# Query and output projections of a two-layer transformer on one core: eleven unit passes computed as seven half products of 128 columns, with the weights' sums kept in DRAM and loaded per visit

## The chip, the cores and the metric

The kernel runs on one core of a Trainium2 chip. The metric is the device time of one execution in microseconds (us). Five engines work side by side, each on its own list of instructions in program order: TensorE (PE, with its weight loads listed apart as PEld), VectorE (DVE), ScalarE (ACT), GpSimd (POOL) and SyncE (SP), which here only issues DMAs. They wait for one another through semaphores.

## The reference

2048 tokens (32 sequences of 64) with 512 features go through two conditioned layers, all in float32. Cut to what matters here:

```python
# layer 0
h = ada_rms(x, cond, ln1_w, ln1_tw)
q = (h @ Wq.T)  ; k = h @ Wk.T ; v = h @ Wv.T        # 8 query heads of 64, one key/value head
ctx = softmax(rope(q) @ rope(k).T / 8) @ v            # within each sequence of 64
x = x + ctx @ Wo.T                                    # Wq, Wo: 512 x 512
h = ada_rms(x, cond, ln2_w, ln2_tw)
x = x + (silu(h @ Wg.T) * (h @ Wu.T)) @ Wd.T          # 512 -> 2048 -> 512
# layer 1
h = layernorm(x) * (1 + scale(cond)) + shift(cond)
q = h @ Wq.T ; c = h @ Wkd.T ; k = c @ Wku.T ; v = c @ Wvu.T   # 16 heads of 32, 4 key/value heads
x = x + softmax(rope(q) @ rope(k).T / sqrt(32)) @ v @ Wo.T     # Wq, Wo: 512 x 512
```

Four projections are square: q and o of both layers. They are what the change touches.

## The kernel before

**Units and blocks.** The tokens are cut into NU = 8 units of UT = 256. Activations are kept with the features on the partitions: x of a unit is a tile [128, 4, 256], four chunks of 128 features. The MLP runs over five blocks of units, BLOCKS = ((0), (1, 2), (3, 4), (5, 6), (7)). While the MLP of one block runs, layer 0's attention of the next block's units and layer 1's attention of finished units run beside it.

**The square projections before.** `project` (L626) computes 128 output features of one unit: four matmuls, one for each chunk of the contraction, each with weights [128, 128] and 256 moving columns, summed in PSUM. A whole square projection takes 16 of them. Each float32 matmul leaves two records in the trace, so 32 records. The weights (`wqkv`, `wo0`, `wq1`, `wo1`) are loaded once and stay in SBUF. `query(i)` in `attention0` and in `attention1` projects half of the queries into one PSUM bank, and `rotate` (L634 to L637) makes the rotary embedding from that bank: v (L634) and u (L635) on DVE, a shuffle of v (L636) on DVE, and their sum qT (L637) on POOL. `output` projects the context cT, and adds each half to x on DVE (L682; for the last two units of layer 1, whose order is written by hand, chunk by chunk in L676).

**The MLP's half products.** The MLP's three matrices are already multiplied with seven half products in place of eight (Strassen's scheme in Winograd's form): the weights of a slice are cut into quarters, the moving tile into two halves of tokens by two halves of features, and seven products of sums of quarters replace the eight products of quarters. `multiply` (L1048) issues the four EARLIER products P1, P6, P5, P7 and later the three LATER ones, P2, P3, P4. The PSUM regions of the early products are read between the two, in `partial`: ACT copies one (e, L1063), DVE makes u (L1064) and w (L1065); the later products are then added onto what stays in the banks. For one unit the moving width is 128 columns, for a pair of units 256. The sums of the weights' quarters are made once, in block 0, on DVE (L331 to L333) and POOL (L334), stored to DRAM (`sums`) and loaded again in all later blocks, four slices ahead of use, all on SP's queue. L331 to L334 wait for the raw weights' loads ("stays<-in_wmlp").

**What sets the order.** At the start and at the end the order of PE's work is written by hand (the strings FIRST and LAST). In between, pieces of the jobs (an MLP block, layer 0's attention of the next units, the chain of layer 1's attentions of units 0 to 5, called `behind`) are interleaved by a planner: each piece yields a cost and a latency, and the planner takes the job that is the least advanced. The program order on every engine is fixed when the kernel is built. In this middle part attention has two PSUM banks ("at"), the MLP six ("gu"). The layer-1 attention of unit 6 starts in the last block, and it ends together with unit 7's in the hand-written end.

**Norms.** The root and its reciprocal (L567 on ACT, L568 on DVE), h from x (L609, L613 on POOL, L622 on DVE), and hc, the sums of h's quarters that the MLP's moving side needs (L850 to L853 on DVE), stand between a unit's output projection and its MLP.

Of the kernel before, what the change touches and what calls it, by code (L numbers as in the profile page):

```python
# [10 lines left out]
F32 = mybir.dt.float32  # L11
I32 = mybir.dt.int32
AF = mybir.ActivationFunctionType
ALU = mybir.AluOpType
# [32 lines left out]
WARM = 11  # L47
STAY = 13854 - 4 * 128 + 4 * 128 + 4 * 256 + 128 + 4 * 7 * 256 + 4 * 7 * 256
FIRST = "aaaaaaa bb a mm aa bb a bbb aa b mm a bb r aa a m b a bi m b i a | b".replace(" ", "")
# [4 lines left out]
H2 = 4  # L54
MODS = 4

LAST = "aa b aa b iii b aa ii b bb bbb aaaa a b a b aaaa bbbb bb bbbb".replace(" ", "")
# [74 lines left out]
def two_blocks(ctx: ExitStack, tc: tile.TileContext, a: dict, out: bass.AP):  # L132
# [9 lines left out]
    def bank(tag, name):  # L142
        return psum.tile([P, 512], F32, tag=tag, name=name, bufs=BANKS[tag])
# [3 lines left out]
    class Regions:  # L147


        def __init__(self, name, n, ht):  # L150
            self.n, self.ht, self.per = n, ht, 512 // (n * ht)
            self.banks = [
                bank("gu", f"{name}_{i}").rearrange("p (r c t) -> p r c t", c=n, t=ht) for i in range(4 // self.per)
            ]

# [13 lines left out]
    def abank(name):  # L169
        tags = homes["now"]  # L170
        homes["n"] += 1
        return bank(tags[homes["n"] % len(tags)], name)
# [4 lines left out]
    def fixed(shape):  # L177
        n, i = int(np.prod(shape[1:])), stays["at"]
        stays["at"] += n
        assert stays["at"] <= STAY  # L180
        t = stays["all"][:, i : i + n]
        if len(shape) == 2:
            return t
        names = "abc"[: len(shape) - 1]
        return t.rearrange(f"p ({' '.join(names)}) -> p {' '.join(names)}", **dict(zip(names, shape[1:])))
# [69 lines left out]

    wqkv = [fixed([P, KC, 384]), fixed([P, KC, 256])]
    wo0 = fixed([P, KC, D])
    wq1 = fixed([P, KC, D])
    wkd = fixed([P, KC, LAT])
    wkv1 = fixed([P, 2, P])  # L260
    wo1 = fixed([P, KC, D])

# [73 lines left out]
    def done_with(kind, what):  # L336
# [11 lines left out]
        else:  # L348
            load_part(kind, n + MW)

    mods = []

# [13 lines left out]
    load_x(0)  # L366
    for i, w in enumerate(wqkv):
        nc.sync.dma_start(w, a[f"wqkv{i}"])
    load_x(1)
    load_mod(1)  # L370
    nc.sync.dma_start(wo0, a["wo0"])
    first_loads.close()
# [251 lines left out]
    def project(ps, w, cols, h):  # L624
        for k in range(KC):
            nc.tensor.matmul(ps, w[:, k, cols], h[:, k, :], start=(k == 0), stop=(k == KC - 1))  # L626

    def rotate(dst, src, cos, sin, shape, name):

        u, v = (  # L630
            work(tag, [P, 512], f"{tag}_{name}")[:, : shape[1] * shape[2]].rearrange("p (c t) -> p c t", t=shape[2])
            for tag in "uv"
        )
        nc.vector.tensor_tensor(v, src, sin, ALU.mult)  # L634
        nc.vector.tensor_tensor(u, src, cos, ALU.mult)  # L635
        nc.vector.stream_shuffle(v, v, OTHER)  # L636
        nc.gpsimd.tensor_tensor(dst, u, v, ALU.add)  # L637
# [26 lines left out]

    def output(u, cT, w, name, last=False, fine=False):

        x = x_units[u]
        for h in range(2):
            po = abank(f"po_{name}_{h}").rearrange("p (c t) -> p c t", c=2)
            for c in range(2):  # L670
                o = 2 * h + c
                if fine and c:
                    po = abank(f"po_{name}_{h}_{c}").rearrange("p (c t) -> p c t", c=2)
                project(po[:, c], w, slice(o * P, (o + 1) * P), cT)
                if fine:
                    nc.vector.tensor_tensor(x[:, o], x[:, o], po[:, c], ALU.add)  # L676
                    nc.sync.dma_start(out[u][:, o], x[:, o])
                    yield 1.7, 0.0
            if fine:
                continue  # L680
            part = slice(2 * h, 2 * h + 2)
            nc.vector.tensor_tensor(x[:, part], x[:, part], po, ALU.add)  # L682
            yield 3.4, 2.0 * h
            if last:
                nc.sync.dma_start(out[u][:, part], x[:, part])
# [3 lines left out]
    def attention0(u, room):  # L689
# [4 lines left out]
        def query(i):  # L694

            q = abank(f"q0_{u}_{i}").rearrange("p (c t) -> p c t", c=2)
            for c in range(2):
                project(q[:, c], wqkv[i], slice(c * P, (c + 1) * P), h)
            two = [P, 2, UT]

            def turn(cos, sin):
                cos, sin = (t.unsqueeze(1).to_broadcast(two) for t in (cos, sin))
                rotate(qT[:, 2 * i : 2 * i + 2], q, cos, sin, two, f"q0_{u}_{i}")

            return turn

        def keys_values():
            kv = abank(f"kv0_{u}")
            project(kv[:, :UT], wqkv[0], slice(2 * P, 3 * P), h)
            return kv  # L710

        norm = rms(u, s0a, h, room, f"a{u}")
        yield next(norm)
# [20 lines left out]
        qT = tile4(room, "qT", f"qT0_{u}")  # L734
        turn = turn or query(0)
        turn(cos, sin)
        yield 0.0 if lean else 3.4, 0.0

# [20 lines left out]

        query(1)(cos, sin)  # L760
        yield 3.4, 0.0

# [61 lines left out]
        if not lean:  # L824
            contexts([0, 1])
            yield 1.1, 2.5
        yield from output(u, cT, wo0, f"0_{u}")

# [29 lines left out]
    def attention1(u, room):  # L858
# [34 lines left out]
        yield 0.43, 5.5 if slim else 9.0  # L893

        lat = abank(f"lat_{u}")
        project(lat[:, :UT], wkd, slice(0, LAT), h)
# [6 lines left out]

        def query(i):
            q = abank(f"q1_{u}_{i}")
            for c in range(2):
                project(q[:, c * UT : (c + 1) * UT], wq1, slice((2 * i + c) * P, (2 * i + c + 1) * P), h)
                if lean and c == 0:
                    yield 1.7, 0.0
            many = [P, 2 * US, S]  # L910
            rotate(
                qT[:, 2 * i : 2 * i + 2].rearrange("p c (b s) -> p (c b) s", s=S),
                q.rearrange("p (c s) -> p c s", s=S),
                cos.unsqueeze(1).to_broadcast(many),
                sin.unsqueeze(1).to_broadcast(many),
                many,
                f"q1_{u}_{i}",
            )

        def keys_values():  # L920
# [28 lines left out]

        queries = [query(i) for i in range(2)]  # L950
        if early:
# [82 lines left out]
        else:  # L1034
            contexts([0, 1], pTs)
            yield 1.7, 2.0
        yield from output(u, cT, wo1, f"1_{u}", True, lean)

# [198 lines left out]
    rest = [ahead, Job(turning(), 1.0)]  # L1237
    for w, key in ((wq1, "wq1"), (wkd, "wkd"), (wkv1, "wkv1"), (wo1, "wo1")):
        nc.sync.dma_start(w, a[key])
# [86 lines left out]
def _lay(w):  # L1326

    return np.ascontiguousarray(w.T.reshape(-1, P, w.shape[0]).transpose(1, 0, 2))


def _quarters(w, down):


    if down:
        q = w.reshape(2, 2 * P, 2, NP, P).transpose(3, 4, 0, 2, 1)
    else:
        q = w.reshape(2, NP, P, 2, 2, P).transpose(1, 5, 0, 3, 4, 2)
    return q.reshape(NP, P, 4, 2 * P)[:, :, [0, 1, 3, 2]]

# [64 lines left out]
```

## Time and profile before

| | us |
|---|---|
| median of 3 runs (lowest, highest) | 1000.67 (998.11, 1001.54) |
| the profiled execution | 1000.52 |
| its span in the trace | 998.7 |
| TensorE busy | 975.1 |
| VectorE busy | 530.1 |
| GpSimd busy | 428.2 |
| ScalarE busy | 302.0 |

DMA queues moved 132.23 MB in the span, and 16 DMA engines were busy for 39.5% of it. The granted clock of TensorE was 0.997 of full speed.

How to read what follows. A row of groups has line, engine, operation, tiles and shapes, the number of records, then busy us and mean ns of one, then the idle time of the engine just before them and what ended most of it. Matmuls overlap their neighbours, so a mean per record is longer than the distance from one to the next (the pitch); the pitch is read from unbroken runs in the chain of work that ended last, whose pieces have start, length and what ran. A window's row gives the busy time of PE, PEld, DVE, ACT and POOL in a stretch, the clock, the DMA engines' busy share and GB/s. "stays" is the name of the tiles that are kept for the whole kernel, weights above all; "po", "q", "kv", "lat", "gu" and "down" are PSUM banks.

Holes of TensorE before 240 us are ended by several things; the largest of the waits of PE by its releaser are 5.2 us for "issue" and 2.8 us for DVE's "stays" of L332, both ahead of MLP products.

### The profile page before, as it was taken

The numbers are of one execution on the slowest core, as the hardware profiler recorded it, in microseconds if no ns is written. First come the engines' busy times: TensorE is split into PE (matmuls) and PEld (weight loads), VectorE is DVE, ScalarE is ACT, GpSimd is POOL, SyncE is SP. The second block draws the span as 40 slices with busy tenths as digits, with TensorE's granted clock in tenths as the row PEclk, the third lists the DMA queues.
The fourth block names the chain that finished last, engine by engine and source line by source line (L and its number), as shares of the span: only waits on it lengthen the run. The fifth ranks groups of instructions, "written<-read, shape, count | busy, mean of one in ns | idle before, by whom it ended". The sixth has DMA issues, their size and how long they took to land.

```text
span 998.7 us, 17463 instructions
## 1 busy us (share of the span) xinstructions
PE 975.1 (98%) x6710; PEld 852.4 (85%) x6710; DVE 530.1 (53%) x1119; ACT 302.0 (30%) x560; POOL 428.2 (43%) x439
## 2 busy tenths in 40 slices
PE   8899988999999999999999999999999999999998
PEld 7788988888888888887888888888788889999986
DVE  5658787654373442655246372455334643654274
ACT  4453233223214210225214251222313330423132
POOL 3336257335433334435343352454325343844252
PEclk9999999999999999999999999999999999999999
DMA  7837376624222445223232234333323335745401
GB/s 269 310 117 239 130 248 196 208 92 134 69 69 80 137 139 173 90 80 110 78 108 88 73 132 138 115 106 106 96 86 105 132 109 168 246 149 190 138 1 43
DMA packets 82642, 132.23 MB, mean 132 GB/s; under 512 B 8832, under 2 KB 48512, under 8 KB 82176
## 3 DMA queue, kind: packets, MB, share of 16 engines
q1 hardware_dynamic: 82560, 131.12, 39.5%
q8 instruction: 53, 0.87, 0.4%
q14 instruction: 29, 0.24, 0.1%
HBM read 114.31 MB, written 16.78 MB: 131 GB/s over the span
## 4 chain that ended last, share of the span: by engine, by line
PE 87%; DMA 4%; DVE 3%; ACT 1%; POOL 1%; issue 1%; SPq 1%; POOLq 0%; DVEq 0%; ACTq 0%
PE gu L1048 38%; PE down L1048 17%; PE po L626 11%; PE q L626 10%; DMA stays<-in_wmlp 2%; PE pp L661 2%; PE sc L974 2%; PE lat L626 1%; PE kv L626 1%; ACT cT L815 1%; PE cx L805 1%; PE cx L1005 1%; PE sc L784 1%; DMA mod<-in_mod 1%; PE tab L494 1%
## 5 line engine op out<-in xcount | busy, mean ns | idle before, releaser
L1048 PE MATMUL gu<-h,stays 128*128 128x256 f32 (+1 forms) x1280 | 258.5, 340 | 5.9 <-issue 5.2
L1048 PEld LDWEIGHTS gu<-h,stays 128*128 128x128 f32 x1280 | 208.0, 191 | 30.4 <-issue 7.4
L1048 PE MATMUL down<-stays 128*128 128x256 f32 (+1 forms) x1120 | 208.4, 339 | 0.3 <-DVE stays L332 0.3
L1048 PE MATMUL gu<-hc,stays 128*128 128x256 f32 (+1 forms) x960 | 195.4, 338 | 2.8 <-DVE stays L332 2.8
L1048 PEld LDWEIGHTS down<-stays 128*128 128x128 f32 x1120 | 177.2, 190 | 22.4 <-issue 3.6
L1048 PEld LDWEIGHTS gu<-hc,stays 128*128 128x128 f32 x960 | 157.4, 191 | 18.4 <-DVE stays L332 3.0
L626 PE MATMUL q<-h,stays 128*128 128x256 f32 x480 | 110.7, 384 | 0.0
L626 PE MATMUL po<-cT,stays 128*128 128x256 f32 x480 | 107.9, 380 | 1.0 <-ACT cT L815 0.8
L1104 POOL TENSOR_TENSOR stays<-gate,stays 128x768 f32<-128x768 f32 (+1 forms) x40 | 53.8, 1346 | 114.7 <-DVE stays L1093 103.2
L626 PEld LDWEIGHTS po<-cT,stays 128*128 128x128 f32 x480 | 90.3, 190 | 14.4 <-ACT cT L815 2.4
L626 PEld LDWEIGHTS q<-h,stays 128*128 128x128 f32 x480 | 91.4, 192 | 12.6
L1063 ACT COPY e<-gu 128x256 f32<-128x256 f32 (+1 forms) x80 | 26.2, 328 | 172.5 <-PE gu L1048 169.7
L637 POOL TENSOR_TENSOR qT<-u_q,v_q 128x512 f32<-128x512 f32 x30 | 38.2, 1275 | 86.1 <-DVE v_q L636 82.9
L656 POOL TENSOR_TENSOR p<-p,sm 128x512 f32<-128x512 f32 x40 | 41.5, 1057 | 72.3 <-DVE sm L655 66.0
L682 DVE TENSOR_TENSOR x<-x,po 128x512 f32<-128x512 f32 x28 | 19.2, 686 | 90.7 <-PE po L626 90.7
L1064 DVE TENSOR_TENSOR u<-e,gu 128x256 f32<-128x256 f32 (+1 forms) x80 | 28.6, 358 | 53.2 <-ACT e L1063 53.0
L613 POOL TENSOR_TENSOR h<-x,stays 128x1024 f32<-128x1024 f32 x12 | 23.1, 1929 | 68.4 <-DVE x L682 38.4
L1105 POOL TENSOR_TENSOR stays<-stays 128x512 f32<-128x512 f32 (+1 forms) x40 | 45.0, 1126 | 2.9
L568 DVE RECIPROCAL stays<-stays 128x256 f32<-128x256 f32 (+1 forms) x23 | 35.4, 1540 | 19.7 <-ACT stays L567 19.5
L1065 DVE TENSOR_TENSOR w<-u,gu 128x256 f32<-128x256 f32 (+1 forms) x80 | 29.1, 364 | 30.8 <-PE gu L1048 29.6
L1151 POOL TENSOR_TENSOR x<-x,c 128x256 f32<-128x256 f32 x16 | 12.1, 758 | 74.3 <-DVE c L1138 74.3
L1093 DVE TENSOR_TENSOR gate<-gu,u 128x512 f32<-128x512 f32 (+1 forms) x40 | 23.3, 582 | 32.8 <-PE gu L1048 32.5
(230 smaller groups left out, 1266.2 us busy)
## 6 DMA issues: line engine op xcount, KB each, us to landing
stays<-sums SPq DMA_DIRECT2D x96, 384.0 KB, 3.0
stays<-in_wmlp SPq DMA_DIRECT2D x120, 256.0 KB, 2.9
stays<-in_wmlp SPq DMA_DIRECT2D x120, 128.0 KB, 2.5
stays<-sums SPq DMA_DIRECT2D x96, 128.0 KB, 2.3
sums<-stays SPq DMA_DIRECT2D x24, 384.0 KB, 3.8
mod<-in_mod SPq DMA_DIRECT2D x8, 512.0 KB, 6.3
x<-in_x SPq DMA_DIRECT2D x8, 512.0 KB, 6.2
a<-in_wmlp SPq DMA_DIRECT2D x24, 128.0 KB, 3.8
```

What stands on the lines that cost most here:

```text
L568: nc.vector.reciprocal(r, r)
L613: nc.gpsimd.tensor_tensor(by_seq(h), by_seq(x), per_seq(s, u), ALU.mult)
L626: nc.tensor.matmul(ps, w[:, k, cols], h[:, k, :], start=(k == 0), stop=(k == KC - 1))
L637: nc.gpsimd.tensor_tensor(dst, u, v, ALU.add)
L656: nc.gpsimd.tensor_tensor(p8, p8, sm.unsqueeze(2).to_broadcast(wide), ALU.mult)
L1048: nc.tensor.matmul(ps[REGION[p]][:, c], w[:, slot, cols], moving, start=opening and ps.opens(p, c, k), stop=p in LATER, skip_group_check=True,
L1063: nc.scalar.copy(e, ps[0])
L1064: nc.vector.tensor_tensor(u2, e, ps[1], ALU.add)
L1065: nc.vector.tensor_tensor(w2, u2, ps[2], ALU.add)
L1093: nc.vector.tensor_tensor(c12_21, ps.late_pair()[:, :, 0], u2.to_broadcast([P, 2, ht]), ALU.add)
L1104: e.tensor_tensor(act[:, 2:5], gate[:, 1:4], act[:, 2:5], ALU.mult)
L1105: e.tensor_tensor(act[:, 0:4:2], act[:, 2:4], act[:, 1:3], ALU.subtract)
```

## The change

The queries' and the output's projections of layer 0 for units 3 to 7, and of layer 1 for units 0 to 5, are computed as seven half products of 128 moving columns: five and six unit passes with two projections each, 22 projections. The rest keep the 256-column form. A halved projection is two output halves with 7 products of 2 matmuls each, 28 matmuls of 128 columns in place of 16 of 256.

- `halves_of` makes four half sums of the moving tile, three on DVE and one on POOL.
- `halved_products` issues the early products of both output halves, one "at" bank each, with `partial` after each, yields, and then issues the late products. `halved_queries` puts the four quarters into qT (one on DVE from w and P7, one by an ACT copy, a pair on DVE), and `rotate` then reads qT in place of the PSUM bank. `halved_output` adds the quarters onto x, partly on DVE and partly on POOL.
- The four matrices no longer stay in SBUF. Two rings of two tiles [128, 7, 256] hold seven quarters and sums of one matrix each. A *visit* is a stretch of units that use a matrix in a ring: ring 0 has q0 for units 0 to 3, po0 for unit 3, and then q0 and po0 of units 4 to 7 in turn; ring 1 has po0 for units 0 to 2, then q1 and po1 of units 0 to 5 in turn; at the end po1 of units 6 and 7 goes to ring 0 and their q1 to ring 1.
- At a matrix's first halved use, `square_sums` makes its sums: three additions on DVE and one on POOL for each of two halves. When that visit is done, `square_done` stores them to DRAM (896 KB for each half), and each later visit loads 896 KB for each half, issued on SP right after the last late product of the ring's previous visit. Raw loads, of 512 KB, are for first visits and unhalved uses.
- The keys' and values' weights of layer 0 are a tile of their own, `wkv0`.

In DMAs: 36 loads of 896 KB and 8 stores of 896 KB are added; 1024 KB and wqkv loads of the four matrices go, and raw loads of 512 KB come in their place.

The core of the diff:

```diff
+HALVED = (3, 6)
...
-    wqkv = [fixed([P, KC, 384]), fixed([P, KC, 256])]
-    wo0 = fixed([P, KC, D])
-    wq1 = fixed([P, KC, D])
+    wkv0 = fixed([P, KC, P])
...
-    wo1 = fixed([P, KC, D])
+    square = {ring: [fixed([P, 7, 2 * P]) for i in range(2)] for ring in "01"}
...
+    ORDER = ("q0", "po0", "q1", "po1")
+    visits = {"0": [("q0", (0, 1, 2, 3)), ("po0", (3,))], "1": [("po0", (0, 1, 2)), ("q1", (0,)), ("po1", (0,))]}
+    for u in range(4, NU):
+        visits["0"] += [("q0", (u,)), ("po0", (u,))]
+    for u in range(1, HALVED[1]):
+        visits["1"] += [("q1", (u,)), ("po1", (u,))]
+    visits["0"].append(("po1", (6, 7)))
+    visits["1"].append(("q1", (6, 7)))
...
+    def halved(what, u):
+        return u >= HALVED[0] if what[-1] == "0" else u < HALVED[1]
+
+    def load_square(ring, n, i):
+        if n >= len(visits[ring]):
+            return
+        what, units = visits[ring][n]
+        t = square[ring][i]
+        if what in summed_yet and halved(what, units[-1]):
+            nc.sync.dma_start(t, summed[what][:, i])
+        else:
+            nc.sync.dma_start(t[:, 3:7], a["square"][ORDER.index(what), i])
...
+    def square_done(what, u, i):
+        ring, n = visit_of[what, u]
+        if u == visits[ring][n][1][-1]:
+            if halved(what, u) and (what, i) not in summed_yet:
+                summed_yet.add((what, i))
+                nc.sync.dma_start(summed[what][:, i], square[ring][i])
+                if i:
+                    summed_yet.add(what)
+            load_square(ring, n + 1, i)
+
+    def square_sums(what, u):
+
+        if what not in summed_yet:
+            for i in range(2):
+                t = square_of(what, u, i)
+                nc.vector.tensor_tensor(t[:, 0], t[:, 6], t[:, 5], ALU.add)
+                nc.vector.tensor_tensor(t[:, 1], t[:, 0], t[:, 3], ALU.subtract)
+                nc.vector.tensor_tensor(t[:, 2], t[:, 3], t[:, 6], ALU.subtract)
+                nc.gpsimd.tensor_tensor(t[:, 6], t[:, 4], t[:, 1], ALU.subtract)
...
+    def halves_of(h, name):
+
+        b11, b12, b21, b22 = (h[:, r, t] for r in (slice(0, 2), slice(2, 4)) for t in (slice(0, HT), slice(HT, UT)))
+        ts = work("half", [P, 4, 2, HT], f"half_{name}", 2)
+        t1_, t2_, t3_, t4_ = (ts[:, k] for k in range(4))
+        nc.vector.tensor_tensor(t1_, b12, b11, ALU.subtract)
+        nc.gpsimd.tensor_tensor(t3_, b22, b12, ALU.subtract)
+        nc.vector.tensor_tensor(t2_, b22, t1_, ALU.subtract)
+        nc.vector.tensor_tensor(t4_, b21, t2_, ALU.subtract)
...
+    def halved_products(what, u, of, early, late):
+
+        pieces = [(0, CHUNKS[k], k) for k in range(2)]
+        some = []
+        for i in range(2):
+            ps = Regions(f"{what}_{u}_{i}", 1, HT, abank)
+            multiply(ps, EARLIER, True, square_of(what, u, i)[:, 0:4], of, pieces)
+            u2, w2 = partial(ps, ("pe", "pu", "pw"), f"{what}_{u}_{i}", 1, HT)
+            early(i, w2[:, 0], ps[3][:, 0])
+            some.append((ps, u2))
+        yield 3.6, 2.0
+        for i, (ps, u2) in enumerate(some):
+            multiply(ps, LATER, False, square_of(what, u, i)[:, 4:7], of, pieces)
+            square_done(what, u, i)
+            late(i, ps[0][:, 0], ps.late_pair()[:, :, 0], u2.to_broadcast([P, 2, HT]))
+        yield 2.7, 0.0
+
+    def halved_queries(what, u, h, qT, turn):
+
+        quarters = [qT[:, 2 * i : 2 * i + 2].rearrange("p c (h t) -> p (c h) t", t=HT) for i in range(2)]
+
+        def early(i, w2, p7):
+            nc.vector.tensor_tensor(quarters[i][:, 3], w2, p7, ALU.add)
+
+        def late(i, c11, pair, u2):
+            nc.scalar.copy(quarters[i][:, 0], c11)
+            nc.vector.tensor_tensor(quarters[i][:, 1:3], pair, u2, ALU.add)
+            turn(i)
+
+        yield from halved_products(what, u, halves_of(h, f"{what}_{u}"), early, late)
+
+    def halved_output(what, u, cT):
...
+        def early(i, w2, p7):
+            c22 = work("pc", [P, HT], f"pc_{what}_{u}_{i}")
+            nc.vector.tensor_tensor(c22, w2, p7, ALU.add)
+            nc.gpsimd.tensor_tensor(quarters[i][:, 3], quarters[i][:, 3], c22, ALU.add)
+
+        def late(i, c11, pair, u2):
+            to = quarters[i]
+            nc.vector.tensor_tensor(to[:, 1:3], to[:, 1:3], pair, ALU.add)
+            nc.vector.tensor_tensor(to[:, 0], to[:, 0], c11, ALU.add)
+            nc.gpsimd.tensor_tensor(to[:, 1:3], to[:, 1:3], u2, ALU.add)
+
+        of = halves_of(cT, f"{what}_{u}")
+        yield 0.0, 2.0
+        yield from halved_products(what, u, of, early, late)
+        yield 0.0, 2.5
```

## The prediction

> **What bounds the kernel now.** I read the busy times first, then the shares of the chain that ended last, then the pieces of that chain in order of time, the time by stretches, and what TensorE waited for. From the page, the span, the busy times, the chain's shares and the two groups that the change replaces:
>
> ```profile
> span 998.7 us, 17463 instructions
> ...
> PE 975.1 (98%) x6710; PEld 852.4 (85%) x6710; DVE 530.1 (53%) x1119; ACT 302.0 (30%) x560; POOL 428.2 (43%) x439
> ...
> PE 87%; DMA 4%; DVE 3%; ACT 1%; POOL 1%; issue 1%; SPq 1%; POOLq 0%; DVEq 0%; ACTq 0%
> ...
> L626 PE MATMUL q<-h,stays 128*128 128x256 f32 x480 | 110.7, 384 | 0.0
> L626 PE MATMUL po<-cT,stays 128*128 128x256 f32 x480 | 107.9, 380 | 1.0 <-ACT cT L815 0.8
> ```
>
> TensorE (PE) is idle for 998.7 − 975.1 = 23.6 us only. Less PE work is therefore less time, unless new waits take its place. A mean per record (384 ns) overlaps its neighbours, so it is no price; the pitch is. That is read from unbroken pieces of the chain (start, us, what):
>
> ```profile
> 47.77 7.19 PE po L626 x32
> ...
> 79.30 10.73 PE gu L1048 x96
> ...
> 142.43 6.91 PE po L626 x32
> ```
>
> A projection of 256 moving columns is 16 matmuls, two records each: 32 records in 6.91 us, 0.216 us each. The MLP's half products of one unit have 128 columns: 96 records in 10.73 us, 0.1118 us each. Half of 0.216 would be 0.108, so a short record pays 4 ns more than its share.
>
> Where are the 23.6 us? The windows give, for a stretch, its length, then busy us of PE, PEld, DVE, ACT and POOL, the clock, the DMA share and GB/s:
>
> ```profile
> 150.00:165.00 15.00, 11.87 (x98) 11.49 (x97) 9.55 (x26) 6.57 (x11) 13.77 (x16) 0.96 0.52 169
> 165.00:180.00 15.00, 14.72 (x105) 13.94 (x104) 14.93 (x22) 3.05 (x6) 5.86 (x8) 0.92 0.84 259
> 160.00:240.00 80.00, 77.08 (x476) 68.87 (x476) 50.39 (x97) 23.33 (x37) 34.52 (x35) 0.98 0.51 164
> 320.00:400.00 80.00, 80.00 (x399) 69.61 (x398) 31.00 (x56) 13.65 (x24) 32.06 (x30) 1.00 0.44 142
> 880.00:940.00 60.00, 60.00 (x549) 57.22 (x548) 26.09 (x73) 16.04 (x39) 22.23 (x29) 1.00 0.56 185
> ```
>
> From 240 to 940 us PE has no hole worth naming, with DVE busy for 39% (31.00 of 80) to 43% (26.09 of 60). The holes lie ahead of 240 us, and the worst at the border of block 0 and block 1, where DVE is full (14.93 of 15).
>
> **The change part by part.**
>
> 1. *PE work.* A halved projection has 28 matmuls, 56 records: 56 × 0.1118 = 6.26 us instead of 32 × 0.216 = 6.91, a gain of 0.645 us. Queries and outputs are halved in 5 units of layer 0 and 6 of layer 1: 22 projections, **−14.2 us**. If a short record cost only half (0.108), it would be 0.86 each, −19 us; that end I hold unlikely, as no MLP row shows it. The other end is a pitch of 0.1235 (6.91/56), where nothing is left; no unbroken row of 128 columns is near it.
>
> The row above is the answer to a rule that speaks against the change: the Trainium skill (TensorE: Matmul & The Clock Gate, section "LDWEIGHTS (loading the stationary operand)") prices a weight load by its columns alone, about 107 ns for 128, however few columns move. By it the 24 loads (in records) that each projection gains would cost 24 × 107 = 2.6 us if they showed; the 96 records in 10.73 us say that they lie beside the matmuls but for the 4 ns.
>
> 2. *DVE.* Prices by shape: an addition of 128 columns from PSUM 0.28 us (L1064, L1065), of 256 columns 0.42, of 256 columns with both inputs in SBUF 0.43 (L850) to 0.63 (L333). Halved queries add three half sums (1.3 us) and, for each of two column halves, u, w, c22 and the pair (0.28 × 3 + 0.42 = 1.26): 3.8 us. Outputs add 1.3 + 2 × (1.26 + 0.28) = 4.4 and lose two x+=po (L682) of 0.686: 3.0. Eleven of each is 75 us, and 24 weights' sums at 0.57 (L331 to L333) are 14: DVE goes from 530 to about 620 us, 63% of the span. POOL gains some 11 × (0.8 + 3.4) + 8 × 0.81 = 53 us (L1106, L334, L1155), ACT 66 copies × 0.264 = 17 us. In the middle of the run this is hidden by PE; by itself 0. Three places are not:
>
> 3. *The border of blocks 0 and 1.* The six q1 sums (6 × 0.57 = 3.4 us) and unit 3's three half sums (1.3) come before the reciprocal, h and hc of block 1 in DVE's program; L331 to L333 of the next MLP weights are behind them too. The raw q1 halves (2 × 512 KB) and stores of 896 KB go to SP ahead of the MLP's loads, whose "stays" already end waits here (159.71, 3.40 us). DVE has 5.4 us free at 150 to 165 and none at 165 to 180. Bounds: 0 (all fits into the free part) and 4.7 + 6.2 (a 512 KB load in line, by x's row) = 11. I take **+3**, the 4.7 less a part that fits. The six q0 sums (3.4 us) sit after the first angles at 14 us; PE's clock and POOL's L613 set that stretch, bounds 0 and 3.4, I take **+0.5**.
>
> 4. *From early to late products.* Both banks of the attention wait while ACT copies, DVE makes u and w, and other pieces run on PE. In program order the least that stands between is 1.8 us, usually 2.2 to 5; the need is 0.26 + 3 × 0.28 = 1.1 us. It fits, unless a reciprocal (L568, 1749 ns) or a softmax's 0.68 us row is ahead on DVE. An output's P6 also waits for two half sums (0.86 us) after cT; P1 and the piece put between cover that, except in units 3 and 7. Bounds 0 and 22 × 0.65 (all of the gain); I take **+2.5**, a tenth of a us each.
>
> 5. *Loads.* 36 sums of 896 KB and 8 stores are 40 MB on 132, so 51% of the DMA engines' time instead of 39.5%. A ring is loaded again while PE works 30 us and more on other things; only between po0(3) and q0(4) (about 10 us) and po1(5) and q1 of the last pair (about 8.5) is it tight. The nearest rows are 8.6 us (1024 KB wo) and 6.2 (512 KB): bounds 0 and about 3 us for each; I take **+1** in all. SP waits in line for the last late product; the MLP's loads behind it are four slices ahead, which hides some us. If that cover is gone each visit pays what a late load pays (2.8 to 4.6 us on the chain); I take 0.
>
> 6. *Order.* The planner's order shifts by pieces' costs (3.6 + 2.7 against 6.8), which may open or close holes: ±2, taken 0.
>
> Sum against the profiled run's own 1000.52 us (span 998.7 and 1.8 around it; it lies 0.15 under the median): 1000.5 − 14.2 + 3 + 0.5 + 2.5 + 1 = **993.3 us**.
>
> **The rivals.**
>
> A, *all new work is hidden*: 1000.5 − 14.2 = 986. For it: PE is full for 700 us with DVE at 40%. Against: the border, where DVE is full.
>
> B, *the gain goes into waits*: steps 3 to 5 at about 14 instead of 7, so 997.5 to 1003.5. A late load on the chain at both tight places (3 each), 5 at the border, and 3 in step 4 make 14: 1000.
>
> C, *slower: DVE sets the two halves of every projection*. Place: between P7 and P2, in DVE's line. When u waits behind one reciprocal, 1.75 + 1.1 − 1.8 = 1.05 us of PE is open; if that, or as much in softmax rows, meets each of 22, it is 23 us: 1000.5 − 14.2 + 23 + 4.5 = 1014. The change loses from an average of 0.44 us in each of them (0.65 less the 4.5 us of the other steps over 22). For it: both attention banks are held, so no attention piece can fill the hole, and DVE's line does not reorder. Against: the MLP's pieces stand between, and L1064 waits in the same way for the MLP now, with no hole after 240 us.
>
> D, *it does not do what it says*: halves taken at a pitch over 0.12 because a projection's short run changes weights on each matmul and stands alone between other shapes. 56 × 0.1235 gives no gain, 1004 to 1005 with the same waits. The MLP's records change weights as often, so this is small.
>
> **How the numbers follow.** Forecast (989 to 997.5) 0.47; A (under 989) 0.18; B 0.16; C and D (over 1003.5) 0.16 and 0.03. Two runs of this kernel differ by 3.4 us, so 0.3% (3 us) is about what can be told from no change. Faster: 0.47 + 0.18 = 0.65; same 0.16; slower 0.19. The range goes from the clean gain, 985, past B to 1005, where C's lighter half begins; above it is left 0.15, below 0.04.
>
> **What would show it.** Right: PE busy near 961; q and po in rows of 128x128 at 0.112 us a record; PE idle 30 us, with the growth between 140 and 190 us. For A: PE idle still 24. For B: DMA "stays<-summed" among what ended PE's waits. For C: q and po waiting for DVE sums L1064, L1065 or the half sums, a few tenths twice in each unit pass, and gaps between 240 and 940. For D: pitches over 0.12. The forecast is wrong if PE busy does not fall by about 14, or if the region after 240 us has holes.

## The result and the profile after

The changed kernel takes 1027.79 us (median of 5 runs, 1026.01 to 1028.62) against 1000.67 before: a ratio of 1.0271, with a 95% interval of 1.025 to 1.0293. It is slower by 27 us where 7 us less was forecast. Its profiled execution has a span of 1025.0 us. From its page, the lines that answer to those of before:

```profile
span 1025.0 us, 19074 instructions
...
PE 977.2 (95%) x7238; PEld 865.1 (84%) x7238; DVE 635.8 (62%) x1385; ACT 320.7 (31%) x628; POOL 483.9 (47%) x513
...
PE 74%; DVE 14%; POOL 3%; DMA 3%; ACT 2%; issue 2%; POOLq 0%; SPq 0%; DVEq 0%; ACTq 0%
```

TensorE's share of the chain fell from 87% to 74%, VectorE's rose from 3% to 14%. PE is idle for 1025.0 − 977.2 = 47.8 us, 24 more than before, and its busy time did not fall by 14 us but rose by 2.

The pitch that the gain was worked out from is there. Two unbroken pieces of the chain (start, us, what):

```profile
221.03 3.57 PE q L1202 x32
...
496.77 3.57 PE po L1202 x32
```

3.57 / 32 = 0.1116 us a record, 6.25 us for a projection's 56 where 32 long ones took 6.91. So 14 us of work went and some 40 us of lost time came. Where, the windows show (length, then busy us of PE, PEld, DVE, ACT and POOL, the clock, the DMA share, GB/s):

```profile
150.00:165.00 15.00, 8.12 (x58) 7.96 (x57) 11.05 (x21) 3.01 (x6) 10.16 (x11) 0.82 0.64 225
165.00:180.00 15.00, 14.28 (x105) 13.15 (x104) 14.58 (x25) 5.75 (x8) 10.31 (x13) 0.95 0.79 238
160.00:240.00 80.00, 75.71 (x459) 69.01 (x460) 57.70 (x118) 22.98 (x42) 40.29 (x42) 0.96 0.67 217
320.00:400.00 80.00, 78.12 (x460) 67.67 (x458) 37.09 (x80) 21.92 (x40) 33.90 (x35) 1.00 0.49 161
880.00:940.00 60.00, 58.67 (x547) 56.22 (x553) 38.19 (x94) 22.98 (x50) 35.52 (x38) 1.00 0.74 235
```

The worst stretch is the border of blocks 0 and 1, as forecast, but larger: PE is busy for 8.12 of 15 us. And holes are there after 240 us, where there were none. TensorE's waits by what ended them (us in total, times, longest) name many releasers:

```profile
PE gu L1202 <- issue: 6.9, 1, 6.9
PE pp L782 <- POOL p L777: 5.1, 3, 3.3
PE down L1202 <- DMA stays<-sums: 3.7, 1, 3.7
PE lat L673 <- POOL h L1035: 3.7, 4, 1.8
PE ms_b L610 <- POOL stays L603: 2.9, 1, 2.9
PE gu L1202 <- DVE stays L329: 2.4, 1, 2.4
```

Hardly one of them is a halved projection that waits for its own sums. Two of the longest, at 399 and 154 us, have their origin in VectorE's line; the others were not followed back like this. This is the timeline of VectorE around the hole of 3.7 us at 399 us, with ScalarE's copies, GpSimd's h and TensorE's next product (start, us, engine, line, operation, tiles, count, in brackets the idle time before and what ended it):

```profile
389.22 0.27 DVE L741 TENSOR_TENSOR x<-x,po 128x128 f32<-128x128 f32 x1
...
397.20 0.37 ACT L1217 COPY e_d<-down 128x256 f32<-128x256 f32 x1 [14.98 <-PE down L1202]
...
398.87 0.37 ACT L1217 COPY e_d<-down 128x256 f32<-128x256 f32 x1 [1.30 <-PE down L1202]
399.31 1.91 POOL L660 TENSOR_TENSOR h<-x,stays 128x1024 f32<-128x1024 f32 x1 [7.78 <-DMA x<-in_x]
...
401.25 0.42 DVE L690 TENSOR_TENSOR half_q<-h 128x256 f32<-128x256 f32 x1 [11.76 <-POOL h L660]
...
401.71 0.83 DVE L692 TENSOR_TENSOR half_q<-h,half_q 128x256 f32<-128x256 f32 x1
402.57 0.42 DVE L693 TENSOR_TENSOR half_q<-h,half_q 128x256 f32<-128x256 f32 x1
402.92 0.41 DVE L1218 TENSOR_TENSOR u_d<-e_d,down 128x256 f32<-128x256 f32 x1
...
403.38 6.85 PE L1202 MATMUL down<-stays 128*128 128x256 f32 x18 [3.69 <-DMA stays<-sums]
```

VectorE stands idle for 11.76 us, because the next instruction in its line is a half sum of h, and GpSimd could not make h before the unit's x had landed. Behind it in the line is u_d, the MLP's own reading of a "down" bank, which ScalarE had prepared at 397.57 and 399.24 (the ends of its two copies). It runs after the three half sums, and TensorE, idle since 399.69, goes on at 403.38. (The load of the MLP's sums that the table names landed then too; the kernel without the reloads, below, shows that VectorE is enough for a hole there.) Before the change no work of the queries stood in this line for h: their first work on VectorE came after their matmuls. The same at the border of blocks (VectorE's timeline and TensorE's next product):

```profile
148.57 0.29 DVE L471 TENSOR_TENSOR some<-some 128x128 f32<-128x128 f32 x1
153.24 0.43 DVE L391 TENSOR_TENSOR stays<-stays 128x256 f32<-128x256 f32 x1 [4.38 <-DMA stays<-in_square]
...
160.99 0.27 DVE L1238 TENSOR_TENSOR stays<-w,gu 128x128 f32<-128x128 f32 x1
...
161.37 2.05 PE L1202 MATMUL gu<-h,stays 128*128 128x128 f32 x8 [6.88 <-issue]
```

The first weights' sum of q1 waits 4.38 us for its raw load, with the gate and the MLP's weights' sums of block 0 behind it. From 153.24 on VectorE works without a pause, and TensorE's hole from 154.49 ends 0.1 us after VectorE's reading of a "gu" bank (L1238), though the table has only "issue" for it.

Such holes cost twice. In two stretches at the end of holes and behind them the clock column (the last but two) shows half speed:

```profile
161.00:166.00 5.00, 4.63 (x22) 4.67 (x23) 4.30 (x12) 0.84 (x3) 4.92 (x7) 0.50 0.66 237
402.00:408.00 6.00, 4.62 (x11) 3.42 (x12) 3.30 (x8) 0.00 (x0) 1.71 (x3) 0.50 0.22 79
```

The mean clock is 0.987 against 0.997 before: (1 − 0.987) × 1025.0 = 13.3 us lost against (1 − 0.997) × 998.7 = 3.0. This is an estimate; 3.3 us of the half clock lay inside the two holes (159.6 to 161.4 and 401.9 to 403.4 us), where it took nothing from PE's work, so some 9 of the 10 us are in PE's busy time. They hide more than half of the 14 us that the shorter work saved; some 7 us more by which PE's busy time lies over the forecast 961 were not accounted for.

### The profile page after: what moved, and what is told of

The parts are those of the page before. It is cut to its first block, busy times and chain, and to the rows that moved or that the text cites. A ratio compares the mean times of both kernels' runs of the same rounds, so it can differ in the third digit from the quotient of the medians.

```text
span 1025.0 us, 19074 instructions
## 1 busy us (share of the span) xinstructions
PE 977.2 (95%) x7238; PEld 865.1 (84%) x7238; DVE 635.8 (62%) x1385; ACT 320.7 (31%) x628; POOL 483.9 (47%) x513
## 4 chain that ended last, share of the span: by engine, by line
PE 74%; DVE 14%; POOL 3%; DMA 3%; ACT 2%; issue 2%; POOLq 0%; SPq 0%; DVEq 0%; ACTq 0%
PE gu L1202 31%; PE down L1202 15%; PE po L1202 7%; PE q L1202 5%; PE q L679 3%; PE po L679 2%; DVE v_q L755 2%; PE pp L782 2%; PE sc L1128 1%; PE lat L673 1%; DVE u_q L756 1%; DVE v_q L757 1%; ACT cT L958 1%; PE kv L673 1%; DMA stays<-in_wmlp 1%
## 5 line engine op out<-in xcount | busy, mean ns | idle before, releaser
L1202 PE MATMUL down<-stays 128*128 128x256 f32 (+1 forms) x1120 | 213.9, 344 | 4.6 <-DMA stays<-sums 3.7
L1202 PE MATMUL gu<-hc,stays 128*128 128x256 f32 (+1 forms) x960 | 198.9, 341 | 3.9 <-DVE stays L329 2.4
L1202 PE MATMUL po<-half_po,stays 128*128 128x128 f32 x352 | 46.6, 276 | 1.6 <-DVE half_po L692 1.6
L1202 PE MATMUL q<-half_q,stays 128*128 128x128 f32 x352 | 46.7, 276 | 0.0
L1202 PEld LDWEIGHTS po<-half_po,stays 128*128 128x128 f32 x352 | 42.7, 192 | 2.5 <-DVE half_po L692 2.4
L1309 POOL TENSOR_TENSOR x<-x,u_d 128x256 f32<-128x256 f32 x32 | 23.3, 749 | 43.2 <-DVE x L1307 41.9
L767 DVE TENSOR_REDUCE mx<-sc 128x8 f32<-128x512 f32 (+1 forms) x52 | 31.5, 640 | 19.0 <-PE sc L1128 10.9
L1202 PEld LDWEIGHTS q<-half_q,stays 128*128 128x128 f32 x352 | 43.0, 192 | 0.3
L1307 DVE TENSOR_TENSOR x<-x,down 128x256 f32<-128x256 f32 x48 | 18.1, 413 | 34.4 <-PE down L1202 34.3
L1251 ACT ACTIVATE gate<-gate 128x768 f32<-128x768 f32 (+1 forms) x40 | 28.5, 713 | 33.6 <-DVE gate L1247 33.4
```

What stands on the lines that cost most here:

```text
L767: nc.vector.tensor_reduce(mx, s3, AX.X, ALU.max)
L1202: nc.tensor.matmul(ps[REGION[p]][:, c], w[:, slot, cols], moving, start=opening and ps.opens(p, c, k), stop=p in LATER, skip_group_check=True,
L1251: nc.scalar.activation(gate[:, 1:4], gate[:, 1:4], AF.Silu)
```

## The experiments

Each was compared with the kernel before on the same chip. In the text behind each, "thousandths" are those of the time of before; a thousandth is 1 us. The changed kernel stands at +27.1.

**1. TensorE's part alone, and the loads.**

```diff
-            u2, w2 = partial(ps, ("pe", "pu", "pw"), f"{what}_{u}_{i}", 1, HT)
-            early(i, w2[:, 0], ps[3][:, 0])
...
-        yield from halved_products(what, u, halves_of(h, f"{what}_{u}"), early, late)
+        yield from halved_products(what, u, quarters_of(h), None, late)   # whole banks, raw quarters
...
-            nc.sync.dma_start(t, summed[what][:, i])     # pe_alone; in pe_loads two loads of other data
```

> The changed kernel with TensorE's part alone: 28 matmuls of 128 columns per halved projection, but no weights' sums, no half sums (the quarters themselves are the moving side), no reading between early and late products, no stores and no reloads of sums; banks are read whole, as before the change (its products are therefore not the reference's). Theory (the gain is there, the waits around it ate it): 1000.5 - 14.2 = 986, 982 to 991. Rival (the short records, the held banks or the new order of pieces cost it by themselves): 1000 or more.

987.56 us, ratio 0.988 (0.9858 to 0.9903). The rival falls. Its page:

```profile
PE 961.6 (98%) x7238; PEld 857.0 (87%) x7238; DVE 529.2 (54%) x1119; ACT 300.9 (31%) x559; POOL 427.4 (43%) x439
```

PE's busy time is 13.5 us shorter than before (975.1), with 528 records more. The gain, the held banks and the planner's new order are all in this kernel, and it is 12 us faster.

> The same with the loads and stores of each visit put back (896 KB per half and visit, in two DMAs of 512 and 384 KB from other data; stores of 512 KB), and nothing on VectorE. Theory (waits of VectorE and GpSimd in the attention chain and at the border of blocks): at most 5 us over pe_alone, 984 to 993. Rival (the 40 MB of sums are the cost): 1000 or more, most of the 27 us.

991.25 us, 0.991 (0.9879 to 0.994). The loads cost about 3 us, which the intervals do not tell from nothing.

> The changed kernel, but the 36 loads of sums are left out (later visits use the weights that are in the ring, so the output is not the reference's). Theory: the hole at 399 us and its half clock go (3.9 + 3.4), so 1017 to 1024. Rival (loads): 1005 or less.

1028.91 us, 1.03 (1.0254 to 1.0346): no gain. Both expectations fail, the rival's by far. The hole at 400 stays, 2.7 us long, and u_d of VectorE ends it; in the changed kernel a load of sums had ended it because it landed 0.5 us after u_d had begun. A releaser's name is that of the last to come; here another wait of nearly the same length stood behind it.

**2. The weights' sums at the border.**

```diff
+            sums_made.append(latest(tc, mybir.EngineType.DVE))       # block 1's half sums
...
-            square_sums("q1", u)
+            with after(tc, mybir.EngineType.DVE, sums_made[1]):
+                square_sums("q1", u)
```

> The changed kernel with one order added: the six sums of q1 come after block 1's half sums in VectorE's line, so nothing stands behind their wait for the raw load. Theory (that wait held up VectorE's line, 4.4 us, and made the hole of 7.0 us at 154 with up to 3.4 us of half clock): 1017 to 1022. Rival (VectorE is just too full there, or the half clock is not linked to holes): within 3 us of 1027.8.

1026.12 us, 1.0267 (1.0238 to 1.0297): not told apart from the change. The hole at 155 shrank from 6.9 to 4.4 us, and the rest of it stayed (4.1 us are there in no_halves too, below). One blocker out of several bought nothing that can be measured.

**3. The half sums: dependency, work or line?** Three kernels take them apart. In the first, they are made and nobody reads them; in the second, they are not made; in the third, they are made from a constant tile, which is always at hand.

```diff
-        return {"B11": b11, "T3": t3_, "B21": b21, "B22": b22, "T1": t1_, "T2": t2_, "T4": t4_}
+        return {"B11": b11, "T3": b12, "B21": b21, "B22": b22, "T1": b12, "T2": b22, "T4": b21}
...
-        nc.vector.tensor_tensor(t1_, b12, b11, ALU.subtract)     # no_halves: all four out
+        nc.vector.tensor_tensor(t1_, at_hand, at_hand, ALU.subtract)     # halves_ready
```

> The changed kernel with the half sums of the moving side still made (VectorE 44 us, GpSimd 20 us), but products that read the quarters themselves, so that nothing waits for the sums (its products are not the reference's). The step from pe_loads (991.3) to the changed kernel (1027.8) is 36 us, all of it work of VectorE, GpSimd and ScalarE. Theory A (products wait for the end of a longer chain): 1010 to 1019. Theory B (the added work takes up the engines' lines and delays all that stands behind it): within 4 us of 1027.8.

1024.22 us, 1.0241 (1.0223 to 1.0259). Theory A falls: at most some 3 of the 27 us come from products that wait for half sums, and the intervals do not tell that from nothing.

> The same without making the half sums at all. Theory A: within 4 us of halves_unused. Theory B: 8 us or more below halves_unused (64 of some 160 us of added VectorE and GpSimd work are out).

1008.77 us, 1.0087 (1.007 to 1.0104). Theory B holds: 15 us go with sums that no one reads.

> As halves_unused (half sums made, no product reads them), but the half sums read a constant tile that lies in SBUF all the time, so no engine's line waits for their input; each stands behind the instruction of its engine that was written before it. The work, its shapes and its SBUF inputs are the same. Theory B1 (a half sum waits at the head of VectorE's line for h or cT, 11.8 us at 389, and all behind it waits too): within 4 us of no_halves, 1005 to 1013. Theory B2 (the work itself and its quarrel with GpSimd over SBUF is the cost): 1018 to 1026. In between, both.

1013.38 us, 1.0151 (1.0112 to 1.0189; one of its four runs took 1020.26, and by the median alone it would be 13 thousandths): nearer to B1. The same additions, as many and as large, cost 6 thousandths when their input is at hand and 15 when they wait for h and cT. VectorE's waits in halves_unused (us in total, times, longest) have these two lines, and in halves_ready no half sum waits at all:

```profile
DVE half_po L690 <- ACT cT L958: 19.2, 5, 8.1
DVE half_q L690 <- POOL h L660: 17.7, 3, 12.1
```

TensorE's holes agree. The one at 399 us is in halves_unused too, where no product reads the sums (4.0 us), and it is gone in halves_ready and in no_halves. One thing besides the wait differs: halves_ready pins each sum behind the instruction of its engine that was written before it, and so they also stand elsewhere in the line. The group that waits 12.1 us in halves_unused and starts at 399.8 runs at 422.1 there, just ahead of the reading of q's bank. Wait and place were not varied apart.

So of the 18 thousandths that the half sums carry (27.1 − 8.7), some 9 are the blocked line, the wait with its place (24.1 − 15.1), some 6 the work itself (15.1 − 8.7) and some 3 products that wait (27.1 − 24.1). The 9 are clear of the intervals.

**4. The queries' second reading.**

```diff
-            late(i, ps[0][:, 0], ps.late_pair()[:, :, 0], u2.to_broadcast([P, 2, HT]))
+            late(i, ps[0][:, 0], ps.late_pair()[:, :, 0], u2.to_broadcast([P, 2, HT]), whole_bank(ps))
...
-            nc.scalar.copy(quarters[i][:, 0], c11)
-            nc.vector.tensor_tensor(quarters[i][:, 1:3], pair, u2, ALU.add)
-            turn(i)
+            turn(i, bank)
```

> The changed kernel, but each halved query rotates its whole PSUM bank, as before the change, after the late products; the reading between early and late products stays, the ScalarE copy and the pair's addition (0.42 us) go, and u and v read PSUM (0.69 each) in place of SBUF (0.94 to 1.04 on the mean, up to 2.3). The queries' values are not the reference's. Theory A with the rotation as its worst part: 1010 to 1018. Rival (the rotation's second reading is a small part): over 1021.

1025.03 us, 1.0252 (1.0237 to 1.0267): not told apart from the change. That the rotation became slower is plain in the changed kernel's groups on VectorE (count, busy us and mean ns), but it is not what sets the time:

```profile
L756 DVE TENSOR_TENSOR u_q<-qT,stays 128x512 f32<-128x512 f32 x12 | 12.5, 1038 | 0.0
L756 DVE TENSOR_TENSOR u_q<-qT,cs 128x512 f32<-128x512 f32 x10 | 8.5, 853 | 0.0
...
L756 DVE TENSOR_TENSOR u_q<-q,cs 128x512 f32<-128x512 f32 x6 | 4.1, 680 | 0.0
```

From PSUM (q) it takes 680 ns, from SBUF (qT) 853 to 1038 on the mean.

**5. Another order, another engine.**

```diff
         for i in range(2):
             ...
             early(i, w2[:, 0], ps[3][:, 0])
-            some.append((ps, u2))
-        yield 3.6, 2.0
-        for i, (ps, u2) in enumerate(some):
+            yield 1.8, 2.0
             multiply(ps, LATER, False, square_of(what, u, i)[:, 4:7], of, pieces)
             ...
+            yield 1.4, 0.0
```

> The changed kernel with each half's early and late products one after the other (early 0, late 0, early 1, late 1, a piece of the planner each) in place of both early and then both late. One attention bank is held at a time, and the first rotation can start 3 us earlier, but u and w have less time. Theory A: 1015 to 1024. Rival (both banks' holding and the order do not matter): within 3 us of 1027.8; or slower, 1031 and more, if the gap between early and late becomes the wait.

1022.94 us, 1.0226 (1.0206 to 1.0245): 4.5 thousandths better, with intervals that just miss each other, as theory A had it. It holds one bank at a time; the border's hole is 8.0 us here all the same.

```diff
-        nc.vector.tensor_tensor(t1_, b12, b11, ALU.subtract)
+        nc.gpsimd.tensor_tensor(t1_, b12, b11, ALU.subtract)     # and t2_, t4_
```

> The changed kernel with all four half sums on GpSimd. h is GpSimd's own last product, so for queries no line waits for another engine; VectorE loses 44 us of work and all waits for h and cT, GpSimd gains some 27 us. Theory B1: 1008 to 1016. Theory B2 (the work costs wherever it stands): 1018 to 1028.

1031.33 us, 1.032 (1.0303 to 1.0338). B1's forecast fails. VectorE's line is free of half sums, but GpSimd is slower at them, and now products wait: the trace has holes before q and po that end with the third of GpSimd's four half sums (L692), the longest 2.5 us. The cost moved from the line behind to the products ahead.

**6. Queries or outputs.**

```diff
-        return u >= HALVED[0] if what[-1] == "0" else u < HALVED[1]
+        return what[0] == "q" and (u >= HALVED[0] if what[-1] == "0" else u < HALVED[1])     # or "p"
```

> Queries alone in half products (11 projections), outputs as before the change, their raw weights loaded per visit. TensorE's gain is half, 7 us. If queries and outputs share the added 41 us (the 27 us over the kernel before, and the gain) evenly: 1000 - 7 + 20 = 1013. If the blocked line is what counts, outputs (half sums waited 30 us for cT) weigh more than queries (22 us for h): 1008 to 1012 here.

1015.46 us, 1.017 (1.014 to 1.0201).

> Outputs alone in half products (11 projections), queries as before the change. Shared evenly: 1013. If the blocked line is what counts: 1013 to 1018. If the rotation that reads SBUF is what counts, which is not in this kernel: under 1005.

1005.01 us, 1.0054 (1.0036 to 1.0072). Not an even share, and the opposite of what the waits of VectorE would say: queries carry three quarters. They have the border of blocks to themselves: q_only's hole there is 7.7 us, po_only's 1.1. In q_only half sums and weights' sums stand in VectorE's line from 144 to 163 us, in po_only the first of them comes at 199. The two holes differ by 6.6 of the 10 us between the kernels; that the border is the whole difference is not shown.

**7. What is left without the half sums.**

```diff
-        if what not in summed_yet:
+        if False:                       # no_sums_no_halves, besides no_halves
```

> no_halves (1008.8) without the weights' sums as well: the 24 additions on VectorE and 8 on GpSimd are out, loads and stores stay at the sizes of pe_loads (its products are not the reference's). Between no_halves and pe_loads (991.3) 17.5 us are open. If the border of blocks is the main part (q1's sums behind their raw load): 997 to 1003. If the reading of banks and the rotation are: 1005 to 1009.

1005.93 us, 1.0067 (1.0045 to 1.009), against no_halves' 1.0087: 2 thousandths, not told apart. The second case was right.

> no_halves with queries rotated from their PSUM banks as before the change (as in rot_bank). If the second reading of the queries (copy, pair, rotation from SBUF with GpSimd in the way) is the main part of the open 17.5 us: 997 to 1002. If it is small, as rot_bank's 2.8 us says with the half sums in place: 1005 to 1009.

1006.70 us, 1.0078 (1.0057 to 1.0098): not told apart from no_halves either.

> pe_loads (991.3) with the reading of both banks between early and late products put back (per half product group an ScalarE copy and three VectorE additions of 128 columns, 0.26 and 3 x 0.28 us), no half sums, no weights' sums, banks read whole after the late products (its products are not the reference's). After no_sums_no_halves and no_halves_rot_bank some 12 us have no cause. If the late products' wait for these readings is it: 1000 to 1004. If not, and the outputs' additions onto x on GpSimd and the remaining work in VectorE's line are: 991 to 996.

993.81 us, 0.9929 (0.9904 to 0.9955), 2 thousandths over pe_loads: the reading between early and late products is not it, though VectorE's busy time grew from 529.7 to 564.1 us.

> The complement: the changed kernel with its half sums, weights' sums, loads and stores, but nothing read between early and late products, and banks read whole after the late ones, as before the change (its products are not the reference's). If prices add up, this is 1027.8 less what pe_loads to no_halves shows, 17.5 less the weights' sums' 2.8: 1011 to 1015. If the half sums carry their 19 us by themselves whatever else is there: 1010 to 1013. If most of that 19 exists only together with the other work (the lines are full only together): 996 to 1004.

1020.10 us, 1.02 (1.0159 to 1.0241). Prices do not add up: taking out all reading and writing of quarters gains only 7 thousandths as long as the half sums and weights' sums are there. Set it beside no_sums_no_halves, which has the opposite parts. From the two pages, no_partials first:

```profile
PE 971.4 (96%) x7238; PEld 861.5 (85%) x7238; DVE 585.3 (58%) x1209; ACT 304.0 (30%) x562; POOL 456.5 (45%) x469
```

```profile
PE 968.6 (96%) x7238; PEld 860.0 (85%) x7238; DVE 583.5 (58%) x1295; ACT 320.6 (32%) x627; POOL 455.1 (45%) x483
```

VectorE and GpSimd are busy for the same time within 2 us, the first kernel's ScalarE for 16 us less, and yet it is 13 thousandths slower (intervals apart). So busy time does not set the cost by itself. What differs is which instructions stand in the line. Those of the first kernel come before the products and wait for loads, h and cT; those of the second read what the products have just left. That this is the reason fits the waits above; it was not varied by itself.

**8. Can it be mended?**

```diff
+        yield 0.0, 4.0
+        of = halves_of(h, f"{what}_{u}")
+        yield 0.0, 2.0
...
+        with after(tc, mybir.EngineType.DVE, latest(tc, mybir.EngineType.DVE)):
+            with after(tc, mybir.EngineType.Pool, latest(tc, mybir.EngineType.Pool)):
                 nc.vector.tensor_tensor(t1_, b12, b11, ALU.subtract)
```

> The changed kernel, nothing left out, with three orders changed: a wait of 3 or 4 us in the planner before the half sums are written, the half sums of each engine pinned behind the instruction of that engine that was written last, and q1's weights' sums pinned as in pin_q1. If a half sum at the head of VectorE's line is the larger part of their cost (11 of 19 us by halves_unused and halves_ready): 1010 to 1018. If the written order does not hold them back far enough: within 4 us of pin_q1's 1026.1.

1026.40 us, 1.0269 (1.0249 to 1.0289): no gain, but not for the reason expected. The half sums did move. VectorE's long waits for h are gone from the trace and the hole at 154 is 1.1 us; in their place TensorE waits for the half sums. Its waits (us in total, times, longest):

```profile
PE q L1211 <- POOL half_q L693: 9.7, 6, 2.3
PE po L1211 <- DVE half_po L694: 6.5, 1, 6.5
```

> po_only (1005.0) with the same later half sums, nothing left out. po_only's products waited 6.4 us for half sums, and one hole of 2.4 us was followed by half clock. If these go: 997 to 1002, and it may pass the kernel before. If not: 1003 to 1007.

1004.72 us, 1.0051 (1.0036 to 1.0067): not told apart from po_only. No kernel with all of its work in it passed the one before.

## Why the prediction was wrong

*Step 1, TensorE's work: right.* −14.2 us was the price; pe_alone's PE busy time is 13.5 us below that of before, its time 12 thousandths (9.7 to 14.2).

*Step 2, VectorE and GpSimd, "In the middle of the run this is hidden by PE; by itself 0": this is the step that failed.* The amount was nearly right (620 us forecast, which is 62% of the span and not the 63% written there; 635.8 measured). The cover was wrong. I read from a VectorE that is busy for 40% that there is room for 90 us more. But its line is in order (u_d behind the half sums above), and an addition at its head does not take its 0.43 us alone: it takes until its input lands (11.76 us at the longest), and all behind it waits as long. The prediction did ask what stands behind q1's weights' sums; it did not ask it of the half sums, which need h or cT in all 22 projections and had VectorE idle for them 15 times. They carry 18 thousandths (27.1 with them, 8.7 without), where 0 was taken, and half of that goes with the blocked line.

*Step 3, the border of blocks: right place, wrong size.* +3 was taken. The hole grew from 2.6 us to 6.9, with half clock behind it for longer. The 4.7 us of work was counted and its wait for the raw load (4.38 us on VectorE) was put with the loads in SP's queue, not in VectorE's line. Its price alone cannot be given: with q1's sums pinned later the time did not change measurably.

*Step 4, from early to late products, +2.5: fits.* partials_only against pe_loads gives 2 thousandths, within what cannot be told from none.

*Step 5, loads, +1: within the uncertainty of the 3 that pe_loads shows,* and without the 36 reloads the changed kernel is no faster.

*Step 6, the order, 0:* pe_alone has a new order and gains what its records say. Other orders of the same work (split, pin_halves_q1) moved the time by 0 to 4.5 us.

*A term that was missing:* the clock. The prediction priced a hole by its length. Some 9 us of the loss, by the estimate above, came as half clock at and after holes.

*The rivals.* A (all hidden, 986) and B (waits of 14 us, up to 1003.5) fall with the time. C said that it would be slower because VectorE sets the halved projections, and gave 1014. The engine was right, the place was not: between P7 and P2 there is little to find, as step 4 shows. The larger place is before the first products, and there some 3 of the 18 thousandths are products that wait for the sums; the rest falls on what stands behind the sums, such as the MLP's u_d, or is their own work. D falls by the pitch of 0.1116 (its own sum was off as well: no gain and the 7 us of steps 3 to 5 make 1007.5, not 1004 to 1005).

*What stays open.* In the order in which the parts were put back, in thousandths: TensorE's part −12, loads +3, reading between the products +2, writing of the quarters +14, weights' sums +2, half sums +18. The prices do not add up in another order (no_partials), and the fourth has no cause yet. Between partials_only (−7.1) and no_sums_no_halves (+6.7) lie these 14 thousandths for the writing of the quarters: the queries' copy, pair and rotation from SBUF, the outputs' additions onto x on VectorE and GpSimd. The queries' part was taken out of no_halves and did not show, and po_only, with all that the outputs need, is at +5.4 in all; so neither explains it by itself. Why these cost more together than one by one was not settled. Two of the changed kernel's holes, 3.3 us at 264 and 2.9 us at 286, are not the half sums' work, as they are as long in no_halves. Its waits of TensorE have

```profile
PE pp L776 <- POOL p L771: 4.3, 3, 3.3
...
PE ms_b L610 <- POOL stays L603: 2.9, 1, 2.9
```

and no_sums_no_halves, where the weights' sums are out too, still has the second at 2.9 and the first at 1.5, while partials_only has neither above 0.9. Both end with GpSimd, whose line was not varied by itself. GpSimd and VectorE holding each other up at SBUF (the last section) is a candidate that was not tried by itself either. Each kernel also gets a new order of instructions on all engines from one edit, so differences of 2 to 4 us between two of them should not be put down to the edit alone.

## What to carry to other kernels

Where one engine is full and the others are in order, do not price an added instruction by its duration and the share of free time: ask when its input lands, and what stands behind it in that engine's line by then. Build the kernel that has only the gain (here the matmuls, with raw quarters and whole banks) first; it shows how much the rest may cost, here 12 us for 22 sets of sums. And when a hole appears on the bounding engine, look past the releaser's name to the longest idle stretch of the others just before it.

## What the runs showed of the hardware

Half clock came after shorter holes than I had thought of. In the changed kernel holes of PE of 2.4, 2.9 and 3.3 us were each followed within 1.5 us by a stretch of 3.4 us at half speed, and holes of 1.8 and 1.4 us by none; among the short holes of the start, one of 1.6 us was followed too. With the 6.9 and the 3.7 us hole came 6.8 us of half speed, which began inside the hole, 1.8 and 1.5 us before its end. In the kernel before, a hole of 2.6 us was followed by half clock and one of 2.8 us was not. So a hole of 2 to 4 us may cost some 1.7 to 2.7 us more than its length, by an estimate from these stretches (half of the 3.4 us, or of the 6.8 less 1.5). The Trainium skill (TensorE: Matmul & The Clock Gate, section "What's actually happening") says that the clock falls after an idle window of about 3.4 us, and that these windows run freely. The stretches' length agrees with it; the threshold is lower here, since holes of 2.4 to 2.9 us were enough at times. No run here varied the length of a hole alone.

A product on VectorE with both inputs in SBUF took longer beside GpSimd. In the changed kernel the rotation's products that read qT and a table, both in SBUF, took 630 to 693 ns in the 25 cases without a GpSimd instruction beside them; of the 19 with one, 16 took 0.73 to 2.4 us. With one input in PSUM all 20 took 678 to 692 ns, 10 of them beside GpSimd. The longest (start, us):

```profile
691.57 2.29 POOL L1035 TENSOR_TENSOR h<-h,stays 128x1024 f32<-128x1024 f32 x1 [2.09 <-DVE h L1032]
...
692.01 2.40 DVE L756 TENSOR_TENSOR u_q<-qT,cs 128x512 f32<-128x512 f32 x1
```

The Trainium skill (SBUF — State Buffer, section "Who interferes with whom") says that such an instruction shares a port with a GpSimd instruction that reads SBUF, and that one waits for the other's end. The rows agree. The prediction had left the rotation's cost as it was.
